# Sums of four scan directions, group norms and last stages of a four-layer network: GpSimd and VectorE work moved to ScalarE and TensorE, and the last image's stage split into row blocks

## The chip, the cores and the metric

The kernel runs on one core of one Trainium2 chip. The metric is device time in microseconds of one execution. An engine is called PE (TensorE), ACT (ScalarE), DVE (VectorE), POOL (GpSimd) or SP (the engine whose queue issues the DMAs here).

## The reference

The input is x of shape (4, 96, 64, 64): four images, 96 channels, 4096 pixels. Four residual layers follow each other, each on a group norm of its input with 32 groups of three channels:

```
x = x + L0(gn(x))    # sampled attention, 5x5 depthwise, 1x1 projection
x = x + L1(gn(x))    # four-direction state scan over 192 channels, then norm, 1x1 - 3x3 depthwise - 1x1, squeeze gate
x = x + L2(gn(x))    # 3x3 convolution
x = x + L3(gn(x))    # 1x1s, two depthwise branches, four-direction scan (192 channels), norms, grouped 3x3, channel softmax
```

What matters here is the scan of L1 and L3. The 192-channel image u is read as a sequence of 4096 pixels in four directions: rows, rows backwards, columns, columns backwards. In each direction every channel has 16 states, h = h * exp(d * A) + (d * u) * B, y = sum over states of h * C. The four y, brought back to image order, are summed, layer-normed over 192 channels, gated and projected:

```
y = oy[:, 0] + inv[:, 0] + why + invwhy            # rows, rows back, columns, columns back
y = layernorm_last(y) ; return y * silu(z) @ ow.T  # L3; L1 the same with its own gate
```

Behind it L3 adds a second branch, norms over 96 channels, squeezes to 24 + 24 channels, applies a grouped 3x3 and 1x1s, multiplies by a softmax over the channel means of the whole image, and projects.

## The kernel before

Images are (96 channels on partitions) x 4096 pixels in fp32; 192 channels are two halves h. Per image the layers are cut into stages: `first` (L0, and L1 up to u), `second` (L1 behind its scan, L2, L3 up to u) and `third` (L3 behind its scan: `directions`, then `finish`). Between them stand eight scans, two layers x four images, in the order SCANS. Results pass through DRAM images: u in row and column order (`u_row`, `u_col`), the scan's y (`y_row`, `y_col`; the backward direction adds to what the forward one has stored), residuals and gates.

A scan has 32 groups: 4 directions x 4 chunks of 1024 pixels x 2 halves. A group has 12 units of 128 partitions (8 channels x 16 states) x 1024 pixels, so a scan has 384 units, the loop 3072. A unit is: a DMA that spreads a decay argument over 128 partitions (`rep`, L1827, issued four units ahead), exp of it on ACT (L1835, two ahead), a bf16 product on PE that spreads d*u into PSUM (`bx`), the product with B on DVE (L1849), the state scan on DVE (L1856), the product with C on POOL (L1868), and every third unit the sum over states on PE (`acc`). At the end of a group `output` writes y to DRAM one unit later (L1904). `prepare` makes the next groups' operands, from u, on ACT and POOL (L1771 to L1808). `hs`, the result of the scan, has three buffers, `bx` two, `rep` ten.

The order of all instructions is written out by hand. Beside each scan run the stages of BESIDE: `first` or `second` of another image beside scans 0 to 6, and `third` of images 0, 1 and 2 beside scan 7. The stages are generators: they yield numbers that count roughly as one matrix product each, and `unit` lets them run up to a budget per unit, PACE = 3.5, less 2.1 in the units with a sum over states. What a stage has left near the end of its scan is issued at once. All DMAs but a few at the start go through SP's queue in this order, so a load issued behind another, or behind a store that waits for its data, waits too.

In the loop a stage takes its PSUM from two banks (`one`); alone (`solo`), before and after the loop, it has others. The first image's `first` runs alone ahead of the loop and the last image's `third` alone behind it.

The places that the change touches: `group_norm` (L1039) with eight statistics instructions (L1043) and four scalings (L1066) on DVE; `layer_norm` (L1136) over all eight chunks of 512 pixels, with one root on ACT (L1165) and one reciprocal on DVE (L1167) for all; `directions` (L1379), whose column sums `yc` are added in turned order to the row sums V by 16 POOL instructions (L1391); `finish` (L1563) with its loads of `xz` (L1570), `x2` (L1585) and `o` (L1682), each issued at the point of use; KINDS, in which L3's scan goes rows, rows back, columns, columns back; and the loop.

Of the kernel before, what the change touches and what calls it, by code (L numbers as in the profile page):

```python
# [12 lines left out]
ALU = mybir.AluOpType  # L13
# [25 lines left out]
          (("first", 3),), (("second", 2),), (("second", 3),), (("third", 0), ("third", 1), ("third", 2)))  # L39
# [854 lines left out]
def streams(ctx: ExitStack, tc: tile.TileContext, x, wts, cst, out, wat, cat, flag):  # L894
# [144 lines left out]
    def group_norm(src, dst):  # L1039

        st = small.tile([96, 8, 6], F32, name="gn_st")
# [23 lines left out]
        for j in range(4):  # L1065
            nc.vector.tensor_scalar(dst[:, 16 * j : 16 * j + 16, :], img(src)[:, 16 * j : 16 * j + 16, :],  # L1066
                                    g[:, 0:1], g[:, 1:2], ALU.subtract, ALU.mult)
            yield 1
# [67 lines left out]
    def layer_norm(pool, V, n, gains, each):  # L1136

        acc = held()
        sq = {}

        def add(j):
            for h in range(n):
                mm(acc[:8], cv("means")[:96, n - 1, 7 - j : 15 - j], sq.pop((j, h)),
                   j == 0 and h == 0, j == 7 and h == n - 1)

        for j in range(8):
# [5 lines left out]
            for h in range(n):  # L1152
                nc.vector.tensor_sub(V[:, h, js], V[:, h, js], p1[:96])
                t = pool.tile([96, PCH], F32, name="ln_sq", bufs=2 * n)
                nc.scalar.activation(t, V[:, h, js], AF.Square)
                sq[j, h] = t
            yield n
            if j:
                add(j - 1)
                yield  # L1160
                yield n
        add(7)
        yield
        r = pool.tile([8, PCH], F32, name="ln_r", bufs=1)
        nc.scalar.activation(r, acc[:8], AF.Sqrt, bias=eps[:8])  # L1165
        yield n
        nc.vector.reciprocal(r, r)  # L1167
        yield 3
        for j in range(8):
            js = bass.ts(j, PCH)  # L1170
            p = bank()
            mm(p[:96], ident[:8, j : j + 1].to_broadcast([8, 96]), r)
# [206 lines left out]
    def directions(pool, b):  # L1379

        V = pool.tile([96, 2, L], F32, name="V", bufs=1)
        with tc.tile_pool(name="dirs", bufs=1) as T:
            for h in range(2):
                t = T.tile([96, W, H], F32, name="yc")
# [4 lines left out]
                for j in range(8):  # L1389
                    v = img(V[:, h, bass.ts(j, PCH)])  # L1390
                    nc.gpsimd.tensor_tensor(v, v, t[:, :, 8 * j : 8 * j + 8].rearrange("p a b -> p b a"), ALU.add)  # L1391
                    yield 1
        return V

    def second(b):

        with tc.tile_pool(name="p2x", bufs=1) as PX:
            V = yield from directions(PX, b)
# [157 lines left out]

    def third(b):

        with tc.tile_pool(name="p3x", bufs=1) as PX:
            V = yield from directions(PX, b)  # L1560
            yield from finish(PX, b, V)

    def finish(PX, b, V):  # L1563
        with tc.tile_pool(name="p3", bufs=2) as pool:
            w = staged(pool, "l3_in", "l3_out")

            def gate(j):
                js = bass.ts(j, PCH)
# [515 lines left out]
```

## Time and profile before

| | us |
|---|---|
| median of 3 runs (lowest, highest) | 14916.63 (14892.47, 14927.26) |
| profiled execution, its own time | 14908.91 |
| its span | 14907.1 |
| first state scan starts, last ends | 701.65, 14626.55 |
| behind the last state scan | 280.5 |

| engine | busy us | share of the span |
|---|---|---|
| PE | 12122.0 | 81% |
| DVE | 11789.6 | 79% |
| POOL | 10381.2 | 70% |
| ACT | 8282.7 | 56% |

The mean granted TensorE clock is 0.809 of full speed. The share of busy time is a mean over parts with different limits: the stages differ in what they load on each engine while the scan's own load per unit is constant, so the prediction reads stretches of the loop one by one, cut at ends of the state scan (L1856). In the lines shown there, a group is line, engine, operation, out<-in by tile names, shapes, count, then busy us in all, mean ns of one, idle us of the engine just before and what ended it. A wait line is who waited <- for whom: us in all, times, longest. In the timeline, start, length, engine (q: its queue), line, operation.

### The profile page before, as it was taken

The page shows a single profiled execution, that of the slowest core. Times are in us where ns is not written, and L with a number is a line of the kernel's source. Part 1 is how long each engine was busy: PE and PEld are TensorE (multiplying, and loading weights), DVE is VectorE, ACT ScalarE, POOL GpSimd, SP SyncE. Part 2 cuts the span into 40 slices and gives each one's busy share as a digit, 9 for nine tenths or more (in the row PEclk, how much of TensorE's full clock was granted, in tenths as well). Part 3 has the DMA queues.
Part 4 walks back from the last instruction along what each step waited for, and adds up shares of the span by engine and source line. Part 5 has one row for each costly group of instructions (what it writes and reads, how often), then busy time and mean ns, then how long its engine had stood idle before and what let it go on. Part 6 is the DMA issues. An engine that isn't in the chain of part 4 may idle for free. (4 is left out here: it accounts for less than half of the span.)

```text
span 14907.1 us, 126739 instructions
## 1 busy us (share of the span) xinstructions
PE 12122.0 (81%) x40354; PEld 3289.6 (22%) x40354; DVE 11789.6 (79%) x7685; ACT 8282.7 (56%) x11648; POOL 10381.2 (70%) x4746
## 2 busy tenths in 40 slices
PE   8788985988879797989878886897969888667757
PEld 2322221222212121222212221222212222111111
DVE  0577888888878888779887898888878888767884
ACT  3255564556745566555655555565745567545652
POOL 0166877877868777668776787787768777656672
PEclk9878886988879787879877897897879888666666
DMA  0266788786878778668876788786878878666682
GB/s 9 66 160 161 193 207 196 188 204 173 218 174 203 186 195 199 171 166 204 210 176 157 178 201 216 176 207 175 205 187 195 199 178 219 169 166 166 166 207 66
DMA packets 902135, 2644.28 MB, mean 177 GB/s; under 512 B 107280, under 2 KB 257392, under 8 KB 901456
## 3 DMA queue, kind: packets, MB, share of 16 engines
q1 hardware_dynamic: 900800, 2634.83, 71.4%
q8 instruction: 320, 5.24, 0.2%
q14 instruction: 359, 2.94, 0.1%
q10 hardware_dynamic: 656, 1.27, 0.0%
HBM read 2169.08 MB, written 466.62 MB: 177 GB/s over the span
## 5 line engine op out<-in xcount | busy, mean ns | idle before, releaser
L1868 POOL TENSOR_TENSOR rep<-hs,bc 128x1024 f32<-128x1024 f32 x3072 | 7236.0, 2360 | 3150.8 <-DVE hs L1856 2691.1
L1856 DVE TENSOR_TENSOR_SCAN hs<-rep,carry,bx 128x1024 f32<-128x1024 f32 x2304 | 5401.0, 2344 | 277.1 <-POOL rep L1868 13.7
L1849 DVE TENSOR_TENSOR bx<-bx,bc 128x1024 f32<-128x1024 f32 x3072 | 3720.0, 1211 | 895.4 <-PE bx L948 860.7
L1835 ACT ACTIVATE rep<-rep,l_decay 128x1024 f32<-128x1024 f32 x3072 | 3495.5, 1143 | 929.3 <-DMA rep<-dd 901.8
L948 PE MATMUL bx<-parts,spread 24*128 24x512 bf16 x6144 | 1412.2, 436 | 1806.4 <-DVE hs L1856 1756.9
L948 PE MATMUL acc<-rep,ct 128*32 128x512 f32 x12288 | 2615.7, 735 | 188.9 <-POOL rep L1868 188.9
L1856 DVE TENSOR_TENSOR_SCAN hs<-rep,bx 128x1024 f32<-128x1024 f32 x768 | 1754.5, 2284 | 312.2 <-POOL rep L1868 229.1
L948 PEld LDWEIGHTS <-spread 24*128 24x128 bf16 x6144 | 310.6, 93 | 4279.2 <-DVE hs L1856 2899.2
L948 PE MATMUL one<-band,dg 96*96 96x512 f32 x2304 | 1119.5, 621 | 0.0
L948 PE MATMUL one<-upad,diag 96*96 96x512 f32 x2016 | 1032.0, 649 | 2.7 <-ACT ur L1128 2.7
L948 PEld LDWEIGHTS acc<-rep,ct 128*32 128x32 f32 x12288 | 508.5, 127 | 1976.2 <-issue 1489.2
L948 PE MATMUL one<-qq,kk 96*128 96x512 f32 x1152 | 818.2, 799 | 135.5 <-ACT ex L1248 81.8
L1248 ACT ACTIVATE ex<-one 128x512 f32<-128x512 f32 x576 | 343.0, 595 | 746.3 <-PE one L948 741.5
L948 PE MATMUL one<-pr,ct 6*96 6x512 f32 x1024 | 648.4, 731 | 36.7 <-ACT pr L1740 4.3
L1835 ACT ACT_TABLE_LOAD x470 | 603.0, 1283 | 112.0 <-DMA rep<-dd 104.1
L948 PE MATMUL one<-hp,diag 96*96 96x512 f32 x1152 | 607.2, 665 | 49.3 <-POOL diag L1075 49.3
L948 PE MATMUL one<-vpad,diag 96*96 96x512 f32 x1200 | 586.5, 624 | 0.0
L1864 ACT COPY carry<-hs 128x1 f32<-128x1 f32 x2304 | 408.5, 177 | 316.3 <-DVE hs L1856 315.3
L948 PE MATMUL held<-ex,cols 128*32 128x256 f32 x3072 | 568.8, 451 | 11.7 <-ACT ex L1248 5.7
L948 PE MATMUL held<-ex,vT 128*32 128x256 f32 x3072 | 569.3, 451 | 0.0
L948 PEld LDWEIGHTS one<-band,dg 96*96 96x96 f32 x2304 | 350.4, 166 | 532.5 <-issue 517.3
L948 PEld LDWEIGHTS one<-upad,diag 96*96 96x96 f32 x2016 | 320.7, 173 | 500.4 <-issue 480.0
(3403 smaller groups left out, 13884.4 us busy)
## 6 DMA issues: line engine op xcount, KB each, us to landing
rep<-dd SPq DMA_DIRECT2D x3072, 512.0 KB
parts<-du SPq DMA_DIRECT2D x1024, 144.0 KB
bc<-rows SPq DMA_DIRECT2D x256, 512.0 KB
dd<-delta SPq DMA_DIRECT2D x256, 384.0 KB
du<-cut SPq DMA_DIRECT2D x256, 384.0 KB
us<-urow SPq DMA_DIRECT2D x128, 384.0 KB
du<-cut SPq DMA_DIRECT2D x256, 192.0 KB
yrow<-yo SPq DMA_DIRECT2D x128, 384.0 KB
```

Source lines behind the costliest of these rows:

```text
L948: nc.tensor.matmul(o, lhsT=lhsT, rhs=rhs, start=first, stop=last)
L1248: nc.scalar.activation(last.rearrange("p a b -> p (a b)"), p, AF.Exp, scale=HD**-0.5)
L1835: nc.scalar.activation(a, a, AF.Exp, scale=decay[tag][:, k, NG * h + m : NG * h + m + 1])
L1849: nc.vector.tensor_mul(bx, bx, ready[i // NG][2][:, 0, :])
L1856: nc.vector.tensor_tensor_scan(out=hs, data0=a, data1=bx, initial=carry[:, h, m : m + 1] if c else 0.0, op0=ALU.mult, op1=ALU.add)
L1864: nc.scalar.copy(carry[:, h, m : m + 1], live[i][1][:, CH - 1 : CH])
L1868: nc.gpsimd.tensor_tensor(a, hs, ready[i // NG][2][:, 1, :], ALU.mult)
```

## The change

Six things change together.

1. `directions` no longer adds on POOL. ACT copies the turned 8 columns of `yc` into a tile `yt`, PE adds it to V by two products with the identity in one PSUM bank, and ACT copies the sum back to V. Both halves' loads are issued ahead of the first copy (two `yc` buffers), when the counter `stored` of stored groups says that the scan's last groups are out; until then the stage yields WAIT, which ends the unit's budget.
2. `group_norm` in the loop takes the sums by ACT (`accum_out` of four copies, then of eight squares of the difference) and normalizes on ACT; DVE keeps four small instructions. Alone it is the old code.
3. L3's scan goes columns, columns back, rows, rows back.
4. The last image's third stage becomes `last`: it starts in the loop, behind image 2's, turns the finished column sums into V on ACT, and runs `finish` over four blocks of two chunks, from the bottom rows up, each as soon as its two groups of backward rows are stored. POOL adds the row sums. `layer_norm` works on a block; a grouped convolution chunk runs when its neighbours are there. The channel means, the softmax and the last loop run once at the end, over all eight chunks.
5. `finish` loads `xz`, `x2` and `o` one chunk ahead (`Ahead`); `l3_y2` sits with `pw`, and `low` with `up`, on partitions 96 to 119.
6. PACE is 3.5, 3.7 and 3.2 for scans beside first, second and third stages.

```diff
-          (("first", 3),), (("second", 2),), (("second", 3),), (("third", 0), ("third", 1), ("third", 2)))
+          (("first", 3),), (("second", 2),), (("second", 3),), (("third", 0), ("third", 1), ("third", 2), ("last", 3)))
...
+        if not solo[0]:
+            yield from group_norm_on_scalar(src, dst)
+            return
...
+    def group_norm_on_scalar(src, dst):
+        st = small.tile([96, 8], F32, name="gs_st")
+        for j in range(4):
+            s = src[:, bass.ts(j, CH)]
+            nc.scalar.activation(s, s, AF.Copy, accum_out=st[:, j : j + 1])
+            yield 1
+        mv = small.tile([96, 4], F32, name="gs_mv")
+        nc.vector.tensor_reduce(mv[:, 0:1], st[:, 0:4], AX.X, ALU.add)
+        yield 0.5
+        p = bank()
+        mm(p[:96, 0:1], group[:96], mv[:, 0:1])
+        yield
+        nc.scalar.activation(mv[:, 1:2], p[:96, 0:1], AF.Copy, scale=-1.0 / L)
+        yield 0.5
+        for j in range(8):
+            p = bank()
+            nc.scalar.activation(p[:96], src[:, bass.ts(j, PCH)], AF.Square, bias=mv[:, 1:2], accum_out=st[:, j : j + 1])
+            yield 1
+        nc.vector.tensor_reduce(mv[:, 2:3], st, AX.X, ALU.add)
+        yield 0.5
+        p = bank()
+        mm(p[:96, 0:1], group[:96], mv[:, 2:3])
+        yield
+        nc.scalar.activation(mv[:, 2:3], p[:96, 0:1], AF.Sqrt, bias=eps[:96], scale=1.0 / L)
+        yield 0.5
+        nc.vector.reciprocal(mv[:, 2:3], mv[:, 2:3])
+        nc.vector.tensor_mul(mv[:, 3:4], mv[:, 1:2], mv[:, 2:3])
+        yield 0.5
+        for j in range(4):
+            nc.scalar.activation(dst[:, 16 * j : 16 * j + 16, :], img(src)[:, 16 * j : 16 * j + 16, :], AF.Identity,
+                                 scale=mv[:, 2:3], bias=mv[:, 3:4])
+            yield 1
...
+    def layer_norm(pool, V, n, gains, each, chunks=range(8)):
+        chunks = list(chunks)
+        m = len(chunks)
...
+        nc.scalar.activation(r[:m], acc[:m], AF.Sqrt, bias=eps[:m])
         yield n
-        nc.vector.reciprocal(r, r)
+        nc.vector.reciprocal(r[:m], r[:m])
...
+    def directions(pool, b, tag):
         V = pool.tile([96, 2, L], F32, name="V", bufs=1)
         with tc.tile_pool(name="dirs", bufs=1) as T:
+            full = len(groups) // len(SCANS) * (SCANS.index((tag, b)) + 1)
+            cols = []
             for h in range(2):
-                t = T.tile([96, W, H], F32, name="yc")
+                while stored[0] < full - 1 + h:
+                    yield WAIT
+                t = T.tile([96, W, H], F32, name="yc", bufs=2)
+                cols.append(t)
                 for j in range(4):
                     nc.sync.dma_start(out=t.rearrange("p a b -> p (a b)")[:, bass.ts(j, CH)],
                                       in_=y_col[h][b][:, bass.ts(j, CH)])
                     nc.sync.dma_start(out=V[:, h, bass.ts(j, CH)], in_=y_row[h][b][:, bass.ts(j, CH)])
-                for j in range(8):
-                    v = img(V[:, h, bass.ts(j, PCH)])
-                    nc.gpsimd.tensor_tensor(v, v, t[:, :, 8 * j : 8 * j + 8].rearrange("p a b -> p b a"), ALU.add)
-                    yield 1
+                yield 4
+            def turned(n):
+                y = T.tile([96, PCH], F32, name="yt", bufs=2)
+                nc.scalar.copy(img(y), cols[n // 8][:, :, 8 * (n % 8) : 8 * (n % 8) + 8].rearrange("p a b -> p b a"))
+                return y
+            y = turned(0)
+            for n in range(16):
+                v = V[:, n // 8, bass.ts(n % 8, PCH)]
+                p = bank()
+                mm(p[:96], ident[:96, :96], v, True, False)
+                mm(p[:96], ident[:96, :96], y, False, True)
+                yield
+                nc.scalar.copy(v, p[:96])
+                if n < 15:
+                    y = turned(n + 1)
+                yield 1
         return V
...
+    class Ahead:
+        def __init__(self, load, chunks):
+            self.load, self.left = load, list(chunks)
+            self.next = load(self.left.pop(0))
+        def get(self):
+            t, self.next = self.next, self.load(self.left.pop(0)) if self.left else None
+            return t
...
+    def last(b):
+        with tc.tile_pool(name="p3x", bufs=1) as PX:
+            V = PX.tile([96, 2, L], F32, name="V", bufs=1)
+            per_way = 2 * NCH
+            first_ = len(groups) - 4 * per_way
+            while stored[0] < first_ + 2 * per_way:
+                yield WAIT
+            with tc.tile_pool(name="turn", bufs=1) as T:
+                for h in range(2):
+                    t = T.tile([96, W, H], F32, name="yc")
+                    for j in range(4):
+                        nc.sync.dma_start(out=t.rearrange("p a b -> p (a b)")[:, bass.ts(j, CH)],
+                                          in_=y_col[h][b][:, bass.ts(j, CH)])
+                    yield 1
+                    for j in range(8):
+                        nc.scalar.copy(img(V[:, h, bass.ts(j, PCH)]),
+                                       t[:, :, 8 * j : 8 * j + 8].rearrange("p a b -> p b a"))
+                        yield 1
+            yield from finish(PX, b, V, [(first_ + 3 * per_way + 2 * k + 2, (7 - 2 * k, 6 - 2 * k)) for k in range(NCH)])
...
+            def loaded(name, src, bufs):
+                def load(j):
+                    t = pool.tile([96, PCH], F32, tag=name, name=name, bufs=bufs)
+                    nc.sync.dma_start(out=t, in_=src[b][:, bass.ts(j, PCH)])
+                    return t
+                return load
...
+            todo, there = set(range(8)), {-1, 8}
+            for need, chunks in blocks:
+                while stored[0] < need:
+                    yield WAIT
+                if need:
+                    for h in range(2):
+                        yr = Ahead(loaded("tmp", y_row[h], 3), chunks)
+                        for j in chunks:
+                            v = V[:, h, bass.ts(j, PCH)]
+                            nc.gpsimd.tensor_tensor(v, v, yr.get(), ALU.add)
+                            yield 1
+                xzs = Ahead(loaded("xz", gate3, 2), chunks)
...
+                yield from layer_norm(pool, V, 2, wv("l3_ss_outn_g"), gate, chunks)
+                x2s = Ahead(loaded("tmp", skip3, 3), chunks)
+                for j in chunks:
+                    js = bass.ts(j, PCH)
+                    x2 = x2s.get()
...
+                yield from layer_norm(pool, V[:, 0:1, :], 1, wv("l3_ln_g"), squeeze, chunks)
+                there |= set(chunks)
+                for j in sorted(k for k in todo if k - 1 in there and k in there and k + 1 in there):
+                    todo.remove(j)
...
+            o_s = Ahead(loaded("tmp", res2, 3), range(8))
...
-                o = pool.tile([96, PCH], F32, tag="tmp", name="o")
-                nc.sync.dma_start(out=o, in_=res2[b][:, js])
+                o = o_s.get()
...
-             "l3_": ((0, "r", False), (2, "r", True), (1, "c", False), (3, "c", True))}
+             "l3_": ((1, "c", False), (3, "c", True), (0, "r", False), (2, "r", True))}
...
-    PACE = 3.5
+    PACE = {"first": 3.5, "second": 3.7, "third": 3.2}
...
         while store:
             store.pop()()
+            stored[0] += 1
...
             v = next(self.stage, 0)
+            if v == WAIT:
+                return budget
...
-            if at == per - NG - LEAD - 1:
+            if at == per - NG - LEAD - 1 and s < len(SCANS) - 1:
                 work.run()
-            owed = min(owed, 0.5) + PACE - (2.1 if i % 3 == 1 else 0.0)
+            owed = min(owed, 0.5) + PACE[BESIDE[s][0][0]] - (2.1 if i % 3 == 1 else 0.0)
             owed = unit(i, prep, work, owed)
...
-    Slots(third(SCANS[-1][1])).run()
+    work.run()
```

## The prediction

> **What bounds the kernel now.** I read the windows by scan first, then stretches inside a scan, then the groups, the waits of the odd stretches and the timeline of the end. Cuts lie at ends of the state scan (L1856), of which there are 384 per scan and 3072 in all; I call one such step a unit. Columns: stretch, its length, then busy us (and instructions) of PE, weight loads, DVE, ACT, POOL, then the granted TensorE clock, the DMA share and rate.
>
> ```profile
> 2415.70:4113.20 1697.50, 1419.38 (x4268) 386.98 (x4268) 1422.26 (x895) 1000.87 (x1361) 1293.68 (x586) 0.84 0.78 193
> ...
> 12660.00:14626.50 1966.50, 1321.67 (x3530) 286.91 (x3530) 1548.16 (x1074) 1032.39 (x1474) 1321.31 (x620) 0.68 0.71 175
> 14626.60:14907.10 280.50, 219.43 (x338) 51.71 (x338) 66.58 (x95) 66.69 (x120) 25.27 (x25) 0.68 0.11 31
> ...
> 2415.70:2493.90 78.20, 31.79 (x81) 5.61 (x82) 42.15 (x25) 22.19 (x34) 55.84 (x30) 0.54 0.80 195
> ...
> 2692.50:3161.60 469.10, 460.69 (x1483) 137.36 (x1478) 422.59 (x247) 289.36 (x423) 392.06 (x171) 0.97 0.84 203
> ...
> 4009.80:4113.20 103.40, 58.37 (x193) 12.50 (x191) 85.44 (x51) 58.84 (x63) 78.22 (x34) 0.68 0.86 212
> ...
> 13114.80:13196.30 81.50, 50.42 (x136) 14.29 (x134) 54.03 (x41) 31.11 (x41) 39.13 (x17) 0.73 0.55 139
> ...
> 14264.70:14626.50 361.80, 186.31 (x626) 33.85 (x626) 342.84 (x209) 171.22 (x242) 303.93 (x134) 0.60 0.88 213
> ```
>
> A second-stage scan takes 1697.5 us, the last one (three third stages beside it) 1966.5, and 280.5 us run alone behind it. The floor of a unit is the DVE:
>
> ```profile
> L1868 POOL TENSOR_TENSOR rep<-hs,bc 128x1024 f32<-128x1024 f32 x3072 | 7236.0, 2360 | 3150.8 <-DVE hs L1856 2691.1
> L1856 DVE TENSOR_TENSOR_SCAN hs<-rep,carry,bx 128x1024 f32<-128x1024 f32 x2304 | 5401.0, 2344 | 277.1 <-POOL rep L1868 13.7
> L1849 DVE TENSOR_TENSOR bx<-bx,bc 128x1024 f32<-128x1024 f32 x3072 | 3720.0, 1211 | 895.4 <-PE bx L948 860.7
> ...
> L1391 POOL TENSOR_TENSOR V<-V,yc 96x512 f32<-96x512 f32 x128 | 193.6, 1522 | 178.3 <-DMA yc<-ycol 160.5 <-DMA V<-yrow 17.8
> ...
> L1129 ACT COPY uc<-ur 96x512 f32<-96x512 f32 x128 | 141.0, 1102 | 4.0
> ...
> L1066 DVE TENSOR_SCALAR xn<-xn,gn_g 96x1024 f32<-96x1024 f32 x32 | 37.7, 1194 | 0.3
> ```
>
> 2.34 + 1.21 = 3.55 us; with gaps 3.6. So 384 x 3.6 = 1382 us is the floor of a scan, and all above it (315 us in this one, 584 in the last) is beside-work that shows. Where: the 12 units of the directions take 78.2 us, not 43.2; the depthwise band (120 units) runs at 3.91 with PE busy 98% at clock 0.97, so PE bounds it; the last 24 units take 103.4, not 86.4; the 12 units of a third's last loop 81.5, not 43.2. With no work beside (the last row, 96 units) it is 3.77. The waits of three of these stretches:
>
> ```profile
> DVE hs L1856 <- POOL rep L1868: 31.6, 7, 12.8
> ACT rep L1835 <- DMA rep<-dd: 27.3, 3, 13.9
> POOL V L1391 <- DMA yc<-ycol: 22.2, 2, 11.9
> ...
> PE one L948 <- DMA us<-urow: 14.3, 1, 14.3
> ...
> DVE o L1687 <- DMA o<-res: 14.2, 3, 6.4
> ```
>
> The first three belong to the directions: POOL waits 22 us for the column sums, then adds 16 x 1.52 = 24 us; its times-C products are queued behind and the scan waits for their buffers. At the same time the loads of `rep` stand behind the bulk on the queue.
>
> **The change, part by part** (seven directions calls and 14 group norms lie in the loop; the first image's stage runs alone and keeps its code).
>
> *Directions, 7 calls.* Off: 16 POOL adds. On: per chunk a turned copy on ACT (same strided read as L1129, 1.10) and an ACT copy out of PSUM (0.58, as the 512-wide copies L1110 and L1740): 16 x 1.68 = 27 us; and two fp32 identity products on PE, 0.9 us each at clock 0.97 and 1.4 to 2.0 at 0.5 to 0.7 (the pairs of records of `one<-V,cols` and of the tail). The loads do not shrink: both halves, 6.3 MB, are now issued within about two units, 25 us at the 250 GB/s that the queue reached there, less the four units (14 us) that `rep` is fetched ahead: 11 us stall. The first turned copy waits for them on ACT, and the decays of the next scans are queued behind it. Then 1.5 chunks per unit: PE 3 x 1.2 (I take a value near the high clock[...]) + 1.94 (bare unit, 186.31/96) = 5.5 us against 3.6, 11 units, +18 us, with ACT below that (1.78 + 2.5 = 4.3). So 29 us shows where 35 to 45 (mean 38) did: -9 a call, **-63**. Ends: -25 a call (PE hidden) to +46 (rival 3).
>
> *Group norms, 14.* DVE loses 8 x 0.68 + 4 x 1.19 + small ones, 2.2 among them: 12.7 us, each exposed because DVE is the floor. ACT gains 4 x 1.1 + 8 x 0.63 + 4 x 1.1 + 12 accumulator reads of 0.19 = 15.5 us over 6.4 units (18 yields at 2.8): 2.4 + 1.8 a unit = 4.2, +0.6 a unit, 4 us. -8 each, **-112**; ends 0 and -12.7. [...] The rows are fp32: 1194 ns for 1024 on DVE (L1066) against 1143 ns on ACT (L1835), no penalty. [...]
>
> *Pace 3.7 in the second stage.* 3.0 slots of work a unit, not 2.8: the band's 120 units become 112. PE is full there, so the time falls only by 8 bare PE units (1.94 x 0.60, 1.2 us at full clock), 10 us, and the 8 units run later at 3.6, 29 us: +19 a scan, **+76** for four. What it buys: by the order of the changed program the stage ends at unit 349 of 384, so its u images have landed when the next scan's first products want them; the wait of 14.3 us at each of the four switches goes: **-56**. Pace 3.5 of the first stage is the old one (its work ends 14 units later, still before the switch): nothing.
>
> *Scan 7.* The last loop's `o` is loaded one chunk ahead. 6.4 us waits on DVE held up the store on SP and with it the `rep` fetch; 38 us excess a call, half of it the two waits (14.2, and the `rep` lateness it starts); -18, three times, **-54**. `xz` and `x2` ahead: **-15** (63.6 us of PE waits for `xz` in eight stages, mostly hidden). Pace 3.2 stretches the same work over more units; no engine is full there: nothing; by the order all three thirds end at unit 304. New: image 3's stage for six of eight chunks in the last 80 units. A third's units between directions and last loop showed 117 us for eight chunks, so 88; 16 turned copies fit in ACT's room (1.78 of 3.6) but bring 3.1 MB, 7; 12 POOL adds (1.09 for 512 at L1289 to 1.52) with waits for rows just stored, behind which times-C products queue, 10; two layer norms a block, so 4.5 more reciprocals at 3.34 on DVE, 15, and their chains, 13. That is 133, less the 16 that those units had: **+120** (80 to 150).
>
> *Tail, 280.5 us.* The order puts only block [1, 0] and the final loop behind the last scan. Steps from the timeline:
>
> ```profile
> 14641.67 0.30 SPq L1904 DMA_DIRECT2D ycol<-yo  x1
> ...
> 14648.55 11.84 POOL L1391 TENSOR_TENSOR V<-V,yc 96x512 f32<-96x512 f32 x8 [10.36 <-DMA yc<-ycol]
> ...
> 14687.73 1.28 ACT L1575 ACT_TABLE_LOAD   x1
> 14687.75 3.34 DVE L1167 RECIPROCAL ln_r<-ln_r 8x512 f32<-8x512 f32 x1 [2.96 <-ACT ln_r L1165]
> ```
>
> Product, sums, output 7.2; store to loaded 6.9; two adds 2.6; layer norm of two chunks 9; root and reciprocal 5.6; gates 2 x 5.9; out 2 x 2.7; second norm 6 + 5.4; squeeze 2 x 7; three group convolutions at 3.9, 11.7; softmax 4.3; final loop 29.5 less 5.7 of `o` waits, 24; last store 4.5: 118. **-162**. [...]six more roots make 12 switches[...]. In the trace the load at 14687.73 begins 0.02 us behind the root (14687.03 + 0.68)[...]. I count 1.28.
>
> **Sum**: -63 - 112 + 76 - 56 - 54 - 15 + 120 - 162 = -266 on the profiled span of 14907.1, so 14641. The median of the runs lies 9.5 above that span: 14651.
>
> **The rivals.**
> 1. *DVE relief pays in full.* The directions and norms sit where DVE or POOL alone were late, and PE keeps up at pace 3.7[...]. Directions -18, norms -12.7, pace 0: -126 - 178 - 56 - 54 - 15 + 120 - 162 = -471, 14446. For it: DVE has the most exposed work. Against: PE at 98%.
> 2. *ACT and PE take back what DVE gives.* Directions 0, norms -4, switches -28, last loops -30, `xz` -5, last stage +140: -65, 14852; only the tail pays. For it: ACT's in-order queue holds the decays.
> 3. *Slower: the loads and copies come one after the other.* If the 25 us of bulk find no cover and 16 chunks then go in lockstep (ACT 1.68, PE 2.0), a call costs 25 + 59 = 84 us, not 29: +55 x 7 = 385 on the sum: 15036. It decides from 38 us a call above my figure, that is, when the stretch of 12 units takes 110 us instead of today's 78. Against: ACT and PE work on neighbouring chunks (two `yt`, two banks).
> That the last image's blocks are not done in the loop is excluded by the order of the program.
>
> **Chances.** Forecast 0.60, rival 1 0.20, rival 2 0.14, rival 3 0.06. Range 14440 to 14850: it takes in rival 1 and stops at rival 2, whose far end and rival 3 are left out. Measured times differ by about 0.2%. Faster by more than that: 0.60 + 0.20 + 0.11 = 0.91; within 0.03 (the poor end of rival 2); slower 0.06.
>
> **What would show it.** Directions: their 12 units near 72 us, with the waits for POOL gone and waits of ACT for `yc` and of PE for `yt` in their place; over 110 and rival 3 holds. Norms: DVE busy about 25 us less per stage scan. Pace: the band stretch over 4.0 us a unit with PE full, and 30 units at 3.6 behind it; below 3.95, rival 1. No wait for u at the four switches. Scan 7 near 1963 us; tail near 118. A tail over 160 or a scan 7 over 2050 would break the sum.

## The result

| | before | after |
|---|---|---|
| median of the runs (lowest, highest), us | 14908.06 (14892.47, 14927.26), 4 runs | 14698.2 (14694.76, 14728.91), 4 runs |
| ratio, 95% interval | | 0.9863 (0.9845 to 0.9882) |
| span of the profiled execution | 14907.1 | 14698.9 |
| first state scan starts | 701.65 | 690.3 |
| scans beside first stages (0, 3, 4) | 1714.0, 1705.8, 1717.3 | 1702.1, 1729.8, 1699.8 |
| scans beside second stages (1, 2, 5, 6) | 1697.5, 1713.8, 1707.1, 1702.8 | 1671.1, 1684.1, 1670.0, 1682.2 |
| scan 7 | 1966.5 | 2040.0 |
| behind the last scan | 280.5 | 129.5 |

The change is 1.4% faster, 47 us above the forecast of 14651. On the spans the 208 us are: the start -11, the first stages' scans -5 together, the second stages' -114, scan 7 +74, the end -151. The windows after, cut at ends of the state scan (now L1969), are: scans 0, 1 and 7; the end; in scan 1 the first 12 units, the next 24, the depthwise band (112 units), the last 24; and 12 units around the last loop of the second of scan 7's three third stages. Columns are as before: length, busy us of PE, weight loads, DVE, ACT and POOL, granted clock, DMA share, GB/s.

```profile
690.30:2392.40 1702.10, 1434.16 (x5554) 396.22 (x5554) 1401.05 (x851) 1027.13 (x1490) 1272.14 (x571) 0.80 0.75 186
2392.40:4063.50 1671.10, 1429.44 (x4332) 391.67 (x4332) 1402.15 (x869) 1056.22 (x1454) 1268.82 (x570) 0.86 0.78 196
12529.40:14569.40 2040.00, 1530.97 (x3930) 341.91 (x3930) 1600.03 (x1133) 1206.73 (x1701) 1269.39 (x593) 0.70 0.69 171
14569.40:14698.90 129.50, 88.21 (x132) 21.68 (x130) 29.12 (x41) 23.36 (x40) 4.82 (x3) 0.63 0.12 34
...
2392.40:2460.10 67.70, 53.43 (x118) 12.16 (x118) 42.38 (x25) 37.82 (x54) 39.14 (x17) 0.70 0.94 238
2460.10:2610.10 150.00, 116.32 (x300) 25.66 (x298) 114.15 (x94) 74.17 (x109) 78.86 (x34) 0.76 0.57 140
2663.10:3112.70 449.60, 447.50 (x1438) 136.07 (x1438) 396.76 (x231) 275.29 (x402) 368.30 (x161) 0.99 0.81 199
3968.60:4063.50 94.90, 48.13 (x160) 8.37 (x160) 85.38 (x51) 48.73 (x54) 78.09 (x34) 0.57 0.86 208
13530.10:13605.00 74.90, 51.97 (x153) 13.34 (x145) 53.76 (x44) 32.15 (x52) 39.25 (x17) 0.74 0.63 170
```

The 24 units behind the first 12 of scan 1, in the kernel before:

```profile
2493.90:2633.60 139.70, 108.15 (x268) 22.91 (x266) 112.11 (x91) 65.08 (x95) 85.24 (x38) 0.72 0.63 153
```

In scan 1 DVE is busy 20 us less than before, ACT 55 more, POOL 25 less. The first 12 units take 67.7 us instead of 78.2, but the 24 behind them 150.0 instead of 139.7, so little of that gain is left after 36 units; the band, with PE busy throughout, has 8 units less and is 19.5 us shorter; the last 24 units take 94.9 instead of 103.4, and the stretch with the last loop 74.9 instead of 81.2 (81.5 around the first third stage's). The costliest groups after (line, engine, operation, tiles, count, busy us, mean ns, idle before and its releaser):

```profile
L1981 POOL TENSOR_TENSOR rep<-hs,bc 128x1024 f32<-128x1024 f32 x3072 | 7224.5, 2357 | 3210.5 <-DVE hs L1969 2664.2
L1969 DVE TENSOR_TENSOR_SCAN hs<-rep,carry,bx 128x1024 f32<-128x1024 f32 x2304 | 5401.7, 2344 | 274.0 <-POOL rep L1981 14.8
L1962 DVE TENSOR_TENSOR bx<-bx,bc 128x1024 f32<-128x1024 f32 x3072 | 3723.6, 1212 | 1086.2 <-PE bx L948 1063.5
...
L948 PE MATMUL bx<-parts,spread 24*128 24x512 bf16 x6144 | 1412.7, 435 | 1662.7 <-DVE hs L1969 1608.8
```

The line of the products `bx` in the kernel before:

```profile
L948 PE MATMUL bx<-parts,spread 24*128 24x512 bf16 x6144 | 1412.2, 436 | 1806.4 <-DVE hs L1856 1756.9
```

The unit's own work has not moved; DVE's times-B products stand longer, nearly all of it for PE's `bx` (1086 us, before 895), and PE in turn stands 1663 us ahead of these products (before 1806), nearly all of it for the end of a state scan. PE's idle time ahead of `bx` turned out to matter most. The waits of scan 1's first 12 units, after (who <- for whom: us, times, longest):

```profile
DVE bx L1962 <- PE bx L948: 20.6, 4, 6.9
...
PEld one L948 <- ACT yt L1437: 17.3, 9, 5.9
ACT V L1447 <- PE one L948: 16.1, 6, 4.2
...
PE one L948 <- ACT yt L1437: 7.2, 5, 5.1
```

The waits for POOL are gone. In their place PE waits for the turned copy `yt`, ACT waits for PE before it copies the sum back and makes the next `yt`, and the scan's own products `bx` are queued on PE behind that. On ACT the decays of later units stand behind the same copies; one that starts without idle time before it, behind a wait of 2.63 us for PE:

```profile
2442.39 0.58 ACT L1447 COPY V<-one 96x512 f32<-96x512 f32 x1 [2.63 <-PE one L948]
2442.88 1.09 ACT L1437 COPY yt<-yc 96x512 f32<-96x512 f32 x1
2443.87 1.15 ACT L1948 ACTIVATE rep<-rep,l_decay 128x1024 f32<-128x1024 f32 x1
```

### The profile page after: what moved, and what is told of

Read it like the earlier page. It is cut to its first block, busy times and chain, and to the rows that moved or that the text cites. A ratio compares the mean times of both kernels' runs of the same rounds, so it can differ in the third digit from the quotient of the medians.

```text
span 14698.9 us, 128101 instructions
## 1 busy us (share of the span) xinstructions
PE 12296.5 (84%) x40802; PEld 3348.5 (23%) x40802; DVE 11654.4 (79%) x7509; ACT 8721.7 (59%) x12340; POOL 10204.0 (69%) x4634
## 4 chain that ended last, share of the span: by engine, by line
PE 50%; DVE 20%; ACT 10%; DMA 7%; issue 6%; POOL 5%; SPq 1%; DVEq 0%; POOLq 0%; ACTq 0%
PE one L948 33%; DVE hs L1969 14%; PE acc L948 9%; PE bx L948 6%; DVE bx L1962 5%; DMA rep<-dd 3%; PE held L948 3%; POOL rep L1981 2%; ACT rep L1948 2%; ACT L1948 1%; ACT ex L1287 1%; ACT L1890 1%; DMA xz<-gate 0%; ACT delta L1888 0%; POOL delta L1893 0%
## 5 line engine op out<-in xcount | busy, mean ns | idle before, releaser
L1969 DVE TENSOR_TENSOR_SCAN hs<-rep,carry,bx 128x1024 f32<-128x1024 f32 x2304 | 5401.7, 2344 | 274.0 <-POOL rep L1981 14.8
L1969 DVE TENSOR_TENSOR_SCAN hs<-rep,bx 128x1024 f32<-128x1024 f32 x768 | 1754.7, 2285 | 123.3 <-ACT carry L1977 29.0
L948 PE MATMUL one<-band,dg 96*96 96x512 f32 x2304 | 1075.9, 605 | 0.0
L948 PE MATMUL one<-upad,diag 96*96 96x512 f32 x2016 | 996.4, 632 | 0.0
L948 PE MATMUL one<-pr,ct 6*96 6x512 f32 x1024 | 652.7, 728 | 84.3 <-DVE V L1192 10.4
```

What stands on the lines that cost most here:

```text
L948: nc.tensor.matmul(o, lhsT=lhsT, rhs=rhs, start=first, stop=last)
L1969: nc.vector.tensor_tensor_scan(out=hs, data0=a, data1=bx, initial=carry[:, h, m : m + 1] if c else 0.0, op0=ALU.mult, op1=ALU.add)
```

## The experiments

All times are medians of repeated runs, against 14698 for the changed kernel; ratios are to the kernel before, run beside them. It gave 14909 to 14923 there and 14908 beside the change, so a difference between two kernels from different sets carries some 15 us of doubt.

**Column sums by GpSimd again, all else as changed.**

```diff
-            y = turned(0)
-            for n in range(16):
...
+            for h in range(2):
+                for j in range(8):
+                    v = img(V[:, h, bass.ts(j, PCH)])
+                    nc.gpsimd.tensor_tensor(v, v, cols[h][:, :, 8 * j : 8 * j + 8].rearrange("p a b -> p b a"), ALU.add)
+                    yield 1
```

> The changed kernel with the column sums added by 16 POOL instructions again; loads, waits for stored groups and everything else as changed. The forecast's step (a directions call shows 29 us instead of 38, seven calls) says 63 us more: about 14761. The rival from the two traces (the first 12 units fell from 78 to 68 us but the 24 units behind rose from 140 to 150, so the stall was mostly moved) says 0 to 40 us more: 14700 to 14740. If the POOL adds were the dear part (rival 1 of the forecast), 126 us or more: above 14820.

14605.84 us, ratio to before 0.9789 (0.9772 to 0.9807): 92 us faster than the changed kernel, where all three theories had it slower or equal. Moving the sums to ScalarE and TensorE costs 13 us a call. The first 12 units of scan 1:

```profile
2383.80:2442.70 58.90, 22.14 (x84) 4.19 (x84) 42.11 (x27) 22.61 (x34) 56.04 (x29) 0.62 0.98 247
```

POOL is busy 56 of 58.9 us and yet the stretch is shorter than before the change (78.2) and after it (67.7). The DMA share is 0.98, so neither POOL nor the loads have room left; which of the two sets the time isn't shown. POOL's waits for its column sums come to less than 4.8 us. The next two runs take the loads apart.

**The same with each half's loads right ahead of its adds, into one column buffer; and with two.**

```diff
-                t = T.tile([96, W, H], F32, name="yc", bufs=2)
+                t = T.tile([96, W, H], F32, name="yc", bufs=1)
...
-                yield 4
-            for h in range(2):
                 for j in range(8):
```

The diff is against the kernel with GpSimd's sums and shows the one with one buffer; the other keeps bufs=2. The yields that followed the loads go with them.

> The column sums on GpSimd as in e1_pool_adds (14606), but each half's loads stand right ahead of its adds again, into one column buffer, as before the change. Theory of the loads: what the directions gained in the changed kernel came from the order of the loads (both halves ahead, two buffers), not from ScalarE and TensorE. Then the first 12 units of the seven second scans go from 59 back to about 78 us, and the time to 14720 to 14750. Rival: the new units of the stage, its waits and the pace made them short, and the loads' order is worth little: 60 to 65 us, 14610 to 14650.

> As e7_loads_by_half, with two column buffers instead of one. If the single buffer was the cause (SyncE's queue stood still for it until the first half's last add, with the loads of rep behind it), the first 12 units stay near 60 us and the time near 14610. If the order alone was the cause (the second half's 3.1 MB are issued so late that its adds wait for them), 78 us and 14720 to 14750. Half of each would give about 14670.

One buffer: 14738.34 us, ratio 0.9891 (0.9866 to 0.9916), +132 over the kernel with both loads ahead. Two buffers: 14700.7, 0.9862 (0.9839 to 0.9885). So of the 132 us the order is 95 and the held buffer 38, nearer to "the order alone" than to "the single buffer". The held buffer shows in the kernel before too: at the column loads (L1386) SP's queue stood 108.6 us for POOL's adds, in 8 waits, the longest 21.2. The first 12 units of scan 1 take 83.3 us with two buffers. With one, window and waits:

```profile
2383.40:2469.80 86.40, 39.62 (x100) 7.81 (x100) 44.59 (x30) 25.04 (x39) 62.52 (x33) 0.60 0.71 176
```

```profile
DVE hs L1955 <- POOL rep L1967: 34.9, 6, 15.2
...
POOL V L1435 <- DMA yc<-ycol: 11.3, 1, 11.3
POOL V L1435 <- DMA V<-yrow: 11.1, 1, 11.1
```

POOL stands 22 us for the loads with the times-C products behind it, and DVE waits 35 us for those: the picture of the kernel before, at a DMA share of 0.71. (The 86.4 us are more than the 78.2 of the kernel before; this kernel keeps the new waits for stored groups, pace 3.7 and the other parts of the change; what costs the 8 us isn't shown.) With both halves issued ahead POOL's waits for the same bytes come to less than 4.8 us in these units.

**Turned copies two chunks ahead of their products.**

```diff
-                y = T.tile([96, PCH], F32, name="yt", bufs=2)
+                y = T.tile([96, PCH], F32, name="yt", bufs=3)
...
-            y = turned(0)
+            ys = [turned(0), turned(1)]
...
-                mm(p[:96], ident[:96, :96], y, False, True)
+                mm(p[:96], ident[:96, :96], ys.pop(0), False, True)
...
-                if n < 15:
-                    y = turned(n + 1)
+                if n < 14:
+                    ys.append(turned(n + 2))
```

> The changed kernel with the turned copies two chunks ahead of their products, in three buffers instead of two. Theory of the ping-pong: the sums on ScalarE and TensorE cost 92 us more than GpSimd's adds since each chunk's identity product waits in PE's order for its turned copy, with the products for a later scan behind it, while ScalarE waits for PE before it makes the next one. A copy further ahead takes most of that away: 14610 to 14650, the first 48 units of the second scans from 271 to about 260 us. Rival: what costs is the work itself, 27 us of ScalarE and some 20 us of PE a call in units that have little room for it: 14690 to 14710, no change beyond 0.1%.

14645.99 us, 0.9826 (0.9802 to 0.9849): 52 of the 92 us come back, at the far end of the first theory's range and outside the second's. The first 48 units of scans 1, 2, 5 and 6 fell from 268 to 272 us to 264 to 268, not to 260. Over half of the price of the new sums is the order in which ACT and PE wait for each other.

**Group norms on DVE again.**

```diff
-        if not solo[0]:
-            yield from group_norm_on_scalar(src, dst)
-            return
```

> The changed kernel with the in-loop group norms on DVE again. The forecast's step (8 us a norm, 14 norms) says 112 us more: about 14810. A rival: not the 12.7 us of DVE work but DVE's wait for the image's load ahead of the first state scan is what went, since the first 12 units beside a first stage fell from 5.5 to 4.1 us each, 17 us a call, and the first state scan starts 11 us earlier; then the three first stages give 11 + 17 + 17 and the other eleven norms little: 50 to 80 us more, 14750 to 14780, and nearly all of it in the first 12 units of scans 0, 3 and 4.

14864.33 us, 0.9964 (0.9953 to 0.9976): the norms are worth 166 us, 11.9 each, of DVE's 12.7 (151 us by the ratios). The rival has its part in it and no more: of the 160 us between the two profiles 11 lie ahead of the first state scan (it starts at 701.6 us, after the change at 690.3) and 5, 17 and 16 in the first 12 units of scans 0, 3 and 4; but the four scans beside second stages, of which it expected little, give 29, 23, 26 and 22. Units 168 to 180 of scan 1 show a norm, first with it on DVE, then after the change:

```profile
3184.80:3252.70 67.90, 35.62 (x102) 9.83 (x102) 56.72 (x44) 27.48 (x30) 41.46 (x25) 0.66 0.74 184
```

```profile
3150.00:3203.90 53.90, 26.06 (x88) 5.07 (x88) 43.85 (x32) 37.07 (x55) 40.02 (x25) 0.59 0.93 235
```

DVE loses 12.9 us and the stretch 14.0; ACT gains 9.6 and still has 16.8 us free. The cuts do not hold quite the same work: a norm on ACT yields more, so the stage is less far on, and the second cut has 14 products fewer.

**Pace 3.5 beside the second stages too.**

```diff
-    PACE = {"first": 3.5, "second": 3.7, "third": 3.2}
+    PACE = {"first": 3.5, "second": 3.5, "third": 3.2}
```

> The changed kernel with pace 3.5 beside second stages. The forecast's step (pace costs 19 us a scan where PE is full, and 14 us a switch come back when the stage ends late) says 20 us less: about 14678. By the traces the depthwise band paid only 10 us a scan for the denser order, so pace 3.5 gives 40 back and loses 56 at four switches plus what no longer fits: 16 us more or beyond, 14715 to 14740.

14815.52 us, 0.9932 (0.9915 to 0.995): 117 slower. By the code a changed second stage yields 42 more than an old one (24 in `directions`, 9 in each norm), and at 3.5 it is not done when the scan nears its end; what is left is issued at once. Units 360 to 372 of scan 1, at pace 3.5 and as changed:

```profile
3955.00:4055.60 100.60, 76.75 (x217) 23.82 (x215) 43.25 (x26) 45.19 (x50) 39.26 (x17) 0.82 0.50 131
```

```profile
3968.60:4019.40 50.80, 25.53 (x84) 4.41 (x84) 42.75 (x26) 28.60 (x32) 39.06 (x17) 0.53 0.84 208
```

At 3.5 these 12 units hold 217 products and take 50 us longer, and the wait for the next scan's u is back in full, at pace 3.5 and then as changed (units 360 to 384):

```profile
PE one L948 <- DMA us<-ucol: 16.7, 1, 16.7
```

```profile
PE one L948 <- DMA us<-ucol: 3.9, 1, 3.9
```

In the 360 units ahead of that, pace 3.7 costs 18, 12, 1 and 32 us in scans 1, 2, 5 and 6, 16 in the mean.

**The last image's stage alone behind the loop.**

```diff
-          (("first", 3),), (("second", 2),), (("second", 3),), (("third", 0), ("third", 1), ("third", 2), ("last", 3)))
+          (("first", 3),), (("second", 2),), (("second", 3),), (("third", 0), ("third", 1), ("third", 2)))
...
+    work.run()
     solo[0] = True
     spare.clear()
-    work.run()
+    Slots(third(SCANS[-1][1])).run()
```

> The changed kernel with the last image's third stage behind the loop, in one block, as before the change. The forecast (the tail gives 162, its share in the loop costs 120) says 42 us more: about 14740. By the traces (tail 129.5 instead of 280.5; the last 80 units 416 us where 80 bare ones take 296) 31 us more: 14730. If the work in the loop were hidden, 150 more: 14850. If it is dearer in the loop than alone, no more or less: 14700 or below.

14724.73 us, 0.9871 (0.9852 to 0.9889). In the profiles scan 7 takes 1921.9 instead of 2040.0 (118 less) and the end 287.8 instead of 129.5 (158 more), so the blocks gain 40 us where they act. By the medians they are worth 27 us, by the ratios 12, and the intervals overlap: scans 0 to 6, which the edit doesn't touch, differ by 13 us between the two profiles. A gain of the blocks is not clear of the noise in the whole time.

**Rows loaded where they are used.**

```diff
-            self.next = load(self.left.pop(0))
...
         def get(self):
-            t, self.next = self.next, self.load(self.left.pop(0)) if self.left else None
-            return t
+            return self.load(self.left.pop(0))
```

> The changed kernel with the rows of the last loops (o, res) and of the gates (xz, x2) loaded where they are used, not one chunk ahead. The prediction put 69 us on loading ahead (54 for o in three last loops, 15 for xz and x2): 14767, if DVE's waits for o set the pace of the last loops. Rival, from the traces: with the loads ahead DVE waits for PE in the same place instead, and the stretch of a last loop fell by 6 us, not 18: 14710 to 14740.

14755.13 us, 0.9893 (0.9877 to 0.991): loading ahead is worth 57 us (45 by the ratios), 63 in the profile's scan 7, of which 14, 13 and 13 in the 12 units around each of the three last loops. The edit also takes the lookahead from the row sums of the last image. The forecast of 69 stands better than the reading of one stretch against the other kernel's (6 us each).

**The second piece of a unit ahead of the products for a later scan.** A unit issues up to two pieces of stage work. PE's order was: first piece, state sums, `bx` for the scan two units on, second piece.

```diff
-        if i + 2 < total:
-            drive(i + 2)
         if first_ is work and budget > 0.9:
             rest = work
         if rest is not idle:
             first_.end()
             budget -= rest.begin(budget)
+        if i + 2 < total:
+            drive(i + 2)
```

> The changed kernel (14698) with one move in the order of a unit: the second piece of work of a unit is issued ahead of the products for the scan two units on, not behind them. Theory of the lockstep: in the last loops and in other pieces that DVE finishes, the DVE instruction stands in order ahead of the next scan, and waits for a product that PE does only behind the products for a later scan, which themselves wait for a buffer that the present scan frees. Then the move takes away most of the 10 us of waits of DVE for PE in each last-loop stretch (74.9 to about 60 us for its 12 units), some 50 us in scan 7 and 20 to 30 in each scan before it: 14500 to 14620. Rival: PE is simply full in these units and the products come later for the move, so that B x waits for PE instead: 14690 to 14800, with the band's 112 units no shorter than 449.

14295.18 us, 0.9583 (0.9559 to 0.9607): 403 us faster than the changed kernel, twice what the whole change gave, and far more than I expected. All scans gain: 24, 26, 44, 53, 24, 22, 43 and 144 us. The band does not (3.9 to 4.3 us a unit in both).

The sign that I had named, the last loops, hardly moved: 12 units of scan 7's second one fell from 74.9 to 71.6 us, not to 60. Their waits, as changed and then with the move:

```profile
PE bx L948 <- DVE hs L1969: 18.0, 7, 5.8
...
DVE tmp L1799 <- PE one L948: 10.4, 4, 3.2
...
DVE tmp L1799 <- DMA tmp<-res: 4.1, 2, 3.6
```

```profile
DVE tmp L1799 <- DMA tmp<-res: 9.3, 2, 4.7
PE bx L948 <- DVE hs L1969: 7.6, 4, 2.7
...
DVE tmp L1799 <- PE one L948: 2.5, 2, 2.0
```

DVE's wait of `tmp` for PE fell from 10.4 to 2.5 us, but the wait for the residual's load grew from 4.1 to 9.3 in its place. The largest gains of scan 7 lie behind the directions, where the layer norms run. Its units 216 to 228, window and waits, as changed and then with the move (14 products fewer in the cut):

```profile
13681.70:13762.60 80.90, 65.92 (x171) 14.08 (x170) 55.71 (x43) 45.41 (x67) 41.22 (x27) 0.79 0.64 158
...
PE bx L948 <- DVE hs L1969: 11.2, 5, 4.3
DVE V L1192 <- PE one L948: 11.0, 5, 3.2
```

```profile
13379.60:13443.10 63.50, 53.99 (x157) 12.09 (x156) 55.33 (x43) 41.96 (x62) 41.16 (x27) 0.88 0.79 197
...
PE bx L948 <- DVE hs L1969: 4.4, 4, 3.2
...
DVE V L1192 <- PE one L948: 3.3, 2, 2.3
```

`bx` has two buffers, so the products for scan i+2 wait for the end of scan i. The second piece's product stood behind them, and what DVE does with it stood in DVE's order ahead of scan i+1: DVE waited for a product that PE had not begun before DVE's previous scan ended. With the move both waits of the pair fall together, DVE's for PE and PE's for DVE's scan. Over the whole program, the moved kernel's group of these products:

```profile
L948 PE MATMUL bx<-parts,spread 24*128 24x512 bf16 x6144 | 1357.7, 437 | 1137.2 <-DVE hs L1969 1083.0
```

PE's idle time ahead of them fell from 1663 to 1137 us, 526 less, in a span 383 shorter. On DVE's side the waits of stage work fell: the layer norms' V waits 63 us for PE, not 119, the sums over states in `yo` 147, not 191. DVE's wait for `bx` itself hardly moved (1043 us, as changed 1064). PE was busy 171 us less for the same number of products, at a mean clock of 0.830 and not 0.817; what of the gain the clock brought, and whether the denser order raised it, isn't shown.

**The same move in the kernel before.** The diff is the same.

> The kernel before the change with the same move of the second piece and nothing else. If the lockstep was there before and is independent of the change, the move is worth 350 to 400 us here too: 14510 to 14560. Rival: the change made it (sums and norms moved to engines that wait for each other, more pieces a unit): then 100 to 200 us here, 14710 to 14810.

14539.73 us, 0.9743 (0.9727 to 0.9759): 379 us below the 14918 run beside it. The lockstep was there before, and the change neither made it nor took it away; with the move on both sides the change is worth 245 us, without it 210.

**Combinations.** The move with GpSimd's sums, and the move with turned copies two ahead.

> e1_pool_adds and e5_slot_before_drive in one kernel: the column sums by GpSimd's adds (both halves' loads ahead), and the second piece of a unit ahead of the products for a later scan. If the two are separate causes, their gains of 92 and 403 us add up: 14200 to 14220, the first 12 units of the second scans near 58 us. Rival: what made ScalarE's and TensorE's sums dear was the same lockstep, which the move already takes away: 14270 to 14300, no better than the move alone.

> e8_turn_two_ahead and e5_slot_before_drive in one kernel: the sums stay on ScalarE and TensorE, the turned copies stand two chunks ahead, and the second piece of a unit is issued ahead of the products for a later scan. By order alone, the 72 us that GpSimd's adds still win with the move (14223 against 14295) go when no product waits for a turned copy: 14220 to 14250, the first 12 units of the second scans from 69 to about 62 us. If the sums' own work on ScalarE and TensorE is what costs: 14280 to 14295, 67 to 69 us.

14223.36 us, 0.9536 (0.952 to 0.9552), and 14238.89, 0.9545 (0.9519 to 0.957). Both are faster than the changed kernel, by 3.2 and 3.1%, and can't be told from each other. The first is 3 us above its range: 72 of 92 us were left to gain beside the move. The second lies in its: the first 12 units of scans 1, 2, 5 and 6 fell to 61 to 64 us, against 66 to 71 with the move alone and 59 to 61 with GpSimd. Sums on ScalarE and TensorE need not cost more than GpSimd's; as the change orders them, they do.

## Why the prediction was right, step by step

The total fell inside the range. Part of that is luck: the norms gained 54 us more than forecast, while the directions, scan 7 and the end gained less. The first 12 units of the scans that begin with `directions` in one table (scans 1, 2, 5, 6, 7; us), since the directions are where the steps failed:

| kernel | first 12 units | median |
|---|---|---|
| before | 78.2, 75.7, 78.3, 77.3, 78.2 | 14908 |
| changed | 67.7, 68.7, 66.0, 67.9, 65.2 | 14698 |
| GpSimd's sums, both loads ahead | 58.9, 58.1, 59.9, 61.3, 55.8 | 14606 |
| GpSimd's sums, loads by half, two buffers | 83.3, 81.3, 82.6, 81.8, 71.6 | 14701 |
| GpSimd's sums, loads by half, one buffer | 86.4, 86.6, 86.8, 88.1, 77.9 | 14738 |

The signs that I named: directions near 72 us (67.7, with waits of ACT and PE for each other, not for the loads alone), DVE 25 us less a stage scan (20 in scan 1), the band over 4.0 with PE full (449.6/112 = 4.01, 447.5 busy); PE's wait for the next scan's u at the four switches fell from between 13.6 and 14.3 us to between 3.8 and 4.5, and was not gone; scan 7 and the end were longer than named. The terms of the sum, with what undoing each gave:

| term | forecast | measured |
|---|---|---|
| directions, 7 calls | -63 | -40 (changed against one buffer, loads by half) |
| of it order and buffers of the loads | | -132 |
| of it ACT and PE in POOL's place | | +92 |
| norms | -112 | -166 |
| pace, away from the scan's end | +76 | +63 |
| rows ahead | -69 | -57 |
| last image in the loop | +120 | +118 |
| the end | -162 | -158 (-151 against the kernel before) |

**Directions.** The total was near (-5.7 a call, forecast -9), the reasons were not, so that it came near was luck. (The sum had a slip too: 11 units at 1.9 us over the floor are 21, not 18, which makes -6 a call.) The step "29 us shows where 35 to 45 did" counted the loads as no smaller, only issued earlier, and let the sums' engines carry the gain. The reverse holds: order and buffers gain 19 us a call, the engines lose 13. I costed ACT and PE at 4.3 and 5.5 us a unit as if each could work on; the waits show each standing for the other (17.3 us of weight loads for `yt`, 16.1 us of ACT for PE in 12 units, at a clock of 0.70, before 0.54). Rival 3 named this taking of turns and priced it for the sum of both, 84 us a call; the stretch never came near its 110, since the loads did not stand in series with it. What the engines are worth could be read only from POOL's adds with the loads already there (58.9 us), which no stretch of the trace of before shows.

**Norms.** Mechanism right, size too small: 11.9 each, not 8. The failed term is the 4 us set against DVE's 12.7 for ACT's 2.4 + 1.8 us a unit. ACT had the room, and little of its added work showed. The fp32 rows that I took from the trace held: for 1024 columns the scaling took 1.19 to 1.34 us on DVE (L1066 before) and takes 1.23 us on ACT (L1103 after).

**Pace and the switches.** The cost was right: 16 us a scan, forecast 19. What it buys was seen only in part. I put 56 us on the waits for u at four switches; 3.8 to 4.5 us of each are left, so 40 of the 56 came, and the last 24 units of the four scans fell by 8, 11, 16 and 14 us, 50 together. The failed part is what stood beside it: without the pace the lengthened stage would not fit, at 50 us a scan. In the sum against the kernel before this is no gain, since there the stage was shorter and did fit (59 us for the same 12 units of scan 1); it is a loss avoided, which a count of the added yields against the whole scan's budget would have shown.

**Rows ahead, last image, end.** 57 for 69, 118 for 120, 158 for 162. Of the o term's 54 us 40 is seen. The step that gave half of the 38 us excess a call to o's lateness was a little high, and what stayed was of another kind: 10.4 us of a last loop's waits were DVE's for PE, of which the move takes 8, with 5 more for the load in their place. What stands behind a late `o` shows on SP's queue: in the kernel before it stood 290.4 us at the store (L1689) for DVE's sums with `o`, in 31 waits. Behind DVE's wait of 6.36 us for `o` such a sum ends at 13180.41 us, the store goes out at 13180.44 and the fetch of `rep` behind it at 13180.87. Scan 7 came to 2040, 77 over the 1963 I named; my own terms add up to 1966.5 - 27 - 54 - 15 + 120 = 1990, so 1963 was a slip (it has the directions' 27 twice) and the miss is 50. The last image's blocks have no share in it, since they cost what was forecast. Of the 50, the sums' price there is 24 us (2040.0 against 2016.1 with GpSimd); how much pace 3.2 adds I did not try. The end, 129.5, is 11.5 over: store to load and the final loop came as counted (6.0 and 28.7 us, forecast 6.9 and 28.5), what lies between, the two norms, gates, squeezes, group convolutions and softmax, took 85, not 73.

**What is left over.** Directions, norms, rows, pace and the last image measured one at a time give -40 - 166 - 57 + 63 - 27 = -227, with the 50 us of the switches -277, against -210 for the change. The 67 us between are not assigned. About half of them go when each run is set against the kernel before of its own set; besides, a stage scan may be bound by different engines with one part in or out, so parts need not add, and some of it may be the clock told of below; neither is shown.

**Rivals.** Rival 1 was nearly right on the norms (12.7) and wrong where PE comes in: directions -5.7 for its -18, pace 16 a scan for its 0. That PE would keep up at pace 3.7 was an estimate; the band took 4.01 us a unit, before 3.91. Rival 2 asked for norms of -4 and fell on that. None of the cases had the largest loss that the runs found in it. PE's 1757 us of waiting ahead of `bx` for the ends of scans, in the kernel before, have no term in the prediction. They were one half of a lockstep, and 400 us lay in it.

## What to carry to other kernels

In one engine's order, put nothing that waits for engine A ahead of work whose result A needs next: one such move gave 403 us here and 379 us in the kernel before. Two engines that show long waits for each other in the same stretch (here 11.2 and 11.0 us of 80.9) are worth a swap of two issue lines before any work is moved between engines. When a change moves work and its loads together, try the loads alone (here 132 us gained by the loads, 92 lost by the engines). Added yields have to be counted against the budget of the whole loop, and a pace raised to make room is the price of the added work, not a gain of its own.

## What the hardware showed

The granted TensorE clock differs between stretches of the same work. Scans 3 and 4 run the same stage of two images; 24 units of each (units 120 to 144), in the changed kernel's windows:

```profile
6328.10:6448.10 120.00, 109.49 (x511) 27.34 (x510) 88.84 (x54) 67.17 (x107) 78.52 (x34) 0.77 0.66 162
```

```profile
8055.30:8166.30 111.00, 99.52 (x512) 25.56 (x510) 88.63 (x54) 66.75 (x107) 78.39 (x34) 0.85 0.71 175
```

The same 511 or 512 products took 10 us more at 0.77 than at 0.85, and the stretch 9 more. The kernel before has both kinds too (505 products in 97.4 us at 0.85 in scan 0 and in 108.1 us at 0.77 in scan 4). In scan 3 of the changed kernel five such stretches in a row took 119 to 120 us, in scan 4 four of the same five took 117 to 119 and one 111; that is 13 of the 30 us of scan 3 over scan 4. What grants the clock isn't shown. PE's busy time alone doesn't tell it: the stretch at 0.77 had PE busy for 109.49 of 120.00 us and the one at 0.85 for 99.52 of 111.00, with no pause over 2.3 us in either, while the band with 447.50 of 449.60 got 0.99. In the kernel before, two stretches behind the directions go the other way round, the busier one at half the clock:

```profile
2500.00:2530.00 30.00, 25.00 (x78) 5.82 (x78) 27.11 (x24) 20.62 (x30) 26.78 (x13) 1.00 0.61 163
2550.00:2570.00 20.00, 18.27 (x36) 3.81 (x39) 18.92 (x17) 10.52 (x13) 9.38 (x4) 0.50 0.38 89
```

A table load on ACT (ACT_TABLE_LOAD) took 1.28 us in both traces. At the end of the changed kernel:

```profile
14665.32 0.19 ACT L1762 ACTIVATION_READ_ACCUMULATOR V<-bx 96x1 f32 x1
14665.52 1.28 ACT L1777 ACT_TABLE_LOAD   x1
```

The load begins 0.01 us behind the end of the instruction before it. Of the 1020 loads behind the first in this trace, 846 have less than 0.3 us of idle time on ACT before and behind them together.
